# Scores and v of layer 1 by two levels of seven block products, with the outer additions done by adding transfers

## The chip, the cores and the metric

The kernel runs on one core of a Trainium2 chip. The metric is device microseconds (us) of one execution, all four layers on all eight images; lower is better. Before the change the median of three runs is 1862.45 us (1861.53 to 1862.72).

## The reference, cut to what matters

Four layers follow each other on x of shape (8, 512, 32, 32). An image is a matrix of C = 512 channels by N = 1024 positions. The change is in layer 1:

```
h = group_norm(x)                                  # 512 x 1024
q, k, v = wq h, wk h, wv h
attn = softmax(q^T k / sqrt(C), axis=-1)           # 1024 x 1024
x = x + wp (v attn^T)
```

Layer 0 is an attention without softmax whose result is a small matrix per image, layer 2 a softmax attention with 128 channels, layer 3 a product of signs with a scale and a slope.

## The kernel before

Weights are folded first: `wu` = wk-by-wq and `wo` = wp-by-wv, each 512 x 512, so layer 1 needs only u = wu h, the scores h^T u (one map of 1024 x 1024), v = h^T wo, and the values, v times the exponentials. All of these are float32 matmuls on the tensor engine (PE), with 128 rows contracted at a time.

Every big product is done by **seven block products in place of eight**. The operands are cut into quarters; `sums_of` (L337) makes the sums of one operand's quarters (A11, A12, A22, S1 to S4), `differences_of` (L353) the differences of the other's (B11, B21, B22, T1 to T4). `seven` (L366) runs the seven products and adds them up into the four result quarters: a result that is a partial sum is first moved out of PSUM by the scalar engine (ACT, `move`, L372) and later products are added to it by the vector engine (DVE, `plus`, L378).

Layer 1's u goes one level further since an earlier version: `make_u2` (L643) makes seven outer products, each of which `inner` (L594) does by seven smaller block products. The sums of the outer level are made by **adding transfers**: a DMA issued by GpSimd (POOL) with `accum_op=ALU.add` (L663) that adds one SBUF tile onto another. `prepare_u` (L576) makes the inner differences of h on POOL and loads the inner sums of wu, which `factors_of_u` (L561) has stored in HBM in batch 0.

The images are eight batches; `fast` (L1173) does one from layer 1's scores to layer 3. Its stages are, in order:

- `scores1` (L715): four groups of `seven` with two calls of 128x512 for each product, then exponentials on ACT and their column sums `esum` on DVE (L733 to L736);
- `make_v` (L698): two groups of `seven` with four calls of 128x256 for each product;
- `inverse_sums` (L1111): four narrow matmuls with ones add up `esum`, and the reciprocals go through HBM to all partitions;
- `values1` (L739): differences of the exponentials and sums of v on DVE, then 14 groups of four calls of 128x512; POOL adds results into xt (L769, L795);
- `project2` (L830), `scores2`, `values2`, `close2`, `leave`: layers 2 and 3. `make_u2` of the next batch is stepped between the matmuls of `project2` and `scores2`.

Into scores and v of a batch fall three other things: the second half of layer 3 of the batch before (`leave` in `rest3`), the loading of a further image, and `entering` (L1153), which runs layer 0's last product of the next image into it, with eight DVE additions (L460) and eight statistics (L463).

The order on PE is written out by hand: the stages are generators, and `fast` steps them one after another (`manual_schedule`). On the other engines a scheduler sets the order when the program is built[...]. POOL's DMA issues stand in POOL's order, plain DMAs in SyncE's (SP). [...]

Of the kernel before, what the change touches and what calls it, by code (L numbers as in the profile page):

```python
# [8 lines left out]
F32 = mybir.dt.float32  # L9
# [7 lines left out]
P = 128  # L17
# [70 lines left out]
def kernel(  # L88
# [55 lines left out]
    def half(i):  # L144
        return bass.ts(i, HF)
# [115 lines left out]
    fac_dram = [dram.tile([P, 7, P], F32, name=f"fac_dram{i}") for i in range(7)]  # L261
# [29 lines left out]
    wo = wpool.tile([P, CC, C], F32, tag="wo", name="wo")  # L291
# [5 lines left out]
    so = wpool.tile([P, 3, 2, C // 2], F32, tag="so", name="so")  # L297
# [214 lines left out]
    def make_u(env, hb, got, early=False):  # L512
# [4 lines left out]
        def done():  # L517
            us = env["big"].tile([P, 3, 2, HF], F32, tag="us", name="us")
            got.append(
                sums_of(quarters_of(ut, chunks, [half(0), half(1)]), [us[:, i] for i in range(3)])  # L520
            )
# [39 lines left out]
    def factors_of_u(env):  # L561

        tt = nc.gpsimd.tensor_tensor
        for i, (a, _) in enumerate(pairs):
            w = weights["u"][a]
            a11, a12, a21, a22 = (w[:, k, bass.ts(m, P)] for m in range(2) for k in range(2))
            s = env["small"].tile([P, 4, P], F32, tag="half_a", name="factors")
            tt(s[:, 0], a21, a22, ALU.add)
            tt(s[:, 1], s[:, 0], a11, ALU.subtract)
            tt(s[:, 2], a11, a21, ALU.subtract)  # L570
            tt(s[:, 3], a12, s[:, 1], ALU.subtract)
            nc.sync.dma_start(out=fac_dram[i][:, 0:2], in_=w[:, :, 0:P])
            nc.sync.dma_start(out=fac_dram[i][:, 2], in_=a22)
            nc.sync.dma_start(out=fac_dram[i][:, 3:7], in_=s)
            yield

    def prepare_u(env, hb, i):

        jit = env["jit"]
        fac = jit.tile([P, 7 + i % 2, P], F32, tag=f"fac{i % 2}", name="fac")  # L580
        nc.sync.dma_start(out=fac[:, 0:7], in_=fac_dram[turns[i]])
        b = hb[pairs[turns[i]][1]]
        t = jit.tile([P, 4, QF], F32, tag="jit", name="jit", bufs=2)
        lo, hi = slice(0, QF), slice(QF, HF)
        tt = nc.gpsimd.tensor_tensor
        for k in range(2):
            tt(t[:, k], b[:, k, hi], b[:, 0, bass.ts(k, QF)], ALU.subtract)  # L587
        tt(t[:, 2], b[:, 1, hi], t[:, 0], ALU.subtract)
        tt(t[:, 3], b[:, 1, lo], t[:, 2], ALU.subtract)
        rhs = {  # L590
            "B11": b[:, 0, lo],
            "B21": b[:, 1, lo],
            "B22": b[:, 1, hi],
            "T1": t[:, 0],  # L594
            "T3": t[:, 1],
            "T2": t[:, 2],
            "T4": t[:, 3],
        }
        return fac, rhs

# [50 lines left out]
    def make_u2(env, hb, got, made):  # L651
# [28 lines left out]
        for i, (d, bias, after) in enumerate(how):  # L680
            for j, _ in enumerate(inner(made[i], d, bias)):
                if j == 3:
# [4 lines left out]
                    if i == 6:  # L687
                        us = []
                        for tag, bufs in (("jit", 2), ("fac1", 1), ("jit", 2)):
                            x = env["jit"].tile([P, 2 * HF], F32, tag=tag, name="us", bufs=bufs)  # L690
                            us.append(x.rearrange("p (i n) -> p i n", i=2))
# [23 lines left out]
    def scores1(env, hb, ua, es):  # L715

        scale = float(C) ** -0.5
        esum = env["small"].tile([P, N], F32, tag="esum", name="esum", bufs=1)
        for i in range(NTH):
            lo, hi = (env["e"].tile([P, N], F32, tag="e", name="e") for _ in range(2))  # L720
            es[i], es[NTH + i] = lo, hi
# [5 lines left out]
            yield from seven(  # L727
                term, lo[:, half(0)], hi[:, half(0)], lo[:, half(1)], hi[:, half(1)], exp=scale
            )
            nc.scalar.activation(hi, hi, AF.Exp, scale=scale)  # L730
            nc.scalar.activation(lo[:, half(0)], lo[:, half(0)], AF.Exp, scale=scale)
            if i == 0:
                nc.vector.tensor_tensor(esum, lo, hi, ALU.add)  # L733
            else:
                nc.vector.tensor_tensor(esum, esum, lo, ALU.add)
                nc.vector.tensor_tensor(esum, esum, hi, ALU.add)  # L736
        es.append(esum)

    def values1(env, xt, vt, es, r, more):  # L739
# [8 lines left out]
        s2 = more[:, 0, :].rearrange("p (t c) -> p t c", c=w)  # L748
        t2 = more[:, 1:3, :].rearrange("p i (t n) -> p (i t) n", n=HF)
        e11, e12, e21, e22 = (  # L750
            [es[k * NTH + t][:, half(n)] for t in range(NTH)] for k in range(2) for n in range(2)
# [23 lines left out]
        for t in range(NTH):  # L775
            tt(e12[t], e22[t], e12[t], ALU.subtract)
            tt(t2[:, t, :], e12[t], e11[t], ALU.add)
# [10 lines left out]
        for t in range(NTH):  # L788
            tt(e11[t], e22[t], t2[:, t, :], ALU.subtract)
# [9 lines left out]
        for t in range(NTH):  # L799
            tt(e21[t], e21[t], t2[:, t, :], ALU.subtract)  # L800
        for i in range(2):
            pb = bank()
            group(pb, s2, [t2[:, t, :] for t in range(NTH)], i, True, True)
# [27 lines left out]
    def project2(env, xt, made):  # L831
# [3 lines left out]
        tpg = big.tile([P, 3, N], F32, tag="us", name="tpg")  # L835
        tt, pt = tpg[:, 0:1, :], tpg[:, 1:2, :]
        gt = tpg[:, 2, :].rearrange("p (t c) -> p t c", c=P)
# [273 lines left out]
    def inverse_sums(env, esum, row):  # L1111
# [4 lines left out]
        for q in range(g):  # L1116
            mm(
                out=ps[bass.ts(q, P // g), 0:w],
                lhsT=ones2[:, 0 : P // g],
                rhs=esum[:, bass.ts(q, w)],  # L1120
                start=True,
                stop=True,
                tile_position=(0, q * P // g),
            )
# [45 lines left out]
    rest3 = []  # L1170
    verdict = []

    def fast(env, n, hb, ua):  # L1173
# [11 lines left out]
        es = [None] * NT  # L1185
        for k, _ in enumerate(scores1(env, hb, ua, es)):
# [6 lines left out]
            if n == 0 and k == 2:  # L1193
                weights["o"] = sums_of(quarters_of(wo, chunks, cols2), [so[:, i] for i in range(3)], True)
            if n == 0 and k in (9, 11, 13, 15, 17, 19, 21):
                next(late_u)
            if n == 0 and k == 6:
                tp = quarters_of(sbw["tpg"], chunks, [slice(0, P), slice(P, 2 * P)])
                weights["tp"] = sums_of(tp, [sp[:, i] for i in range(3)], True)
            if k == 8 and more:  # L1200
                ahead = entering(n + 1)


            if k in (10, 13, 20, 27):
                next(ahead, None)
            chore(n == 0 and k in (1, 4, 7, 9, 11, 15, 17, 19, 23, 25))
        esum = es.pop()
        vt = env["big"].tile([P, NT, C], F32, tag="uv", name="vt")
        for k, _ in enumerate(make_v(hb, vt)):
            if k == 3:  # L1210
                r = inverse_sums(env, esum, n)
            if k == 5:
                next(ahead, None)
            chore(k in (1, 7, 10, 13) or n == 0 and k == 4)
        for _ in ahead:
            pass
        scratch = env["big"].tile([P, 3, N], F32, tag="us", name="scratch")
        got = []
        steps = iter(())
        for k, _ in enumerate(values1(env, xt, vt, es, r, scratch)):  # L1220
            chore(k in (2, 7, 9, 11, 13) or n == 0 and k in (8, 10, 12))
# [9 lines left out]
        signs = None  # L1231
        if more:
# [874 lines left out]
```

## Time and profile before

| | |
|---|---|
| median of three runs | 1862.45 us |
| the profiled execution | 1861.81 us |
| its span, first to last instruction | 1859.9 us |
| granted PE clock | 0.999 |
| PE busy | 1840.3 us (99%) |
| DVE, ACT, POOL busy | 1183.0, 569.6, 382.1 us |
| 128x512 float32 matmuls of values1 (L756), 768 + 128 | 336.9 + 56.2 us busy |
| 128x512 matmuls under L427 of layer 1's scores (ut and us with h and hs), 384 + 256 + 128 + 128 | 178.9 + 115.6 + 60.3 + 60.3 us busy |
| 128x256 matmuls under L427 of v (wo and so with h and hs), 384 + 256 + 128 + 128 | 90.1 + 59.3 + 31.0 + 30.2 us busy |
| adding transfers, 28 of 512 KB and 42 of 256 KB | 25.7 MB |

A group of the profile is a line, an engine, an operation and the tiles that it writes and reads; `bank<-ut,h 128x512 x384` are 384 PE instructions that write a PSUM bank from tiles ut and h. Matmuls overlap, so the mean duration of one (594 ns with 512 columns) is longer than what one more adds to the time. Idle time of an engine that isn't the bound costs nothing. The span is 1.9 us shorter than the execution's own time.

### The profile page before, as it was taken

The numbers are of one execution on the slowest core, as the hardware profiler recorded it, in microseconds if no ns is written. First come the engines' busy times: TensorE is split into PE (matmuls) and PEld (weight loads), VectorE is DVE, ScalarE is ACT, GpSimd is POOL, SyncE is SP. The second block draws the span as 40 slices with busy tenths as digits, with TensorE's granted clock in tenths as the row PEclk, the third lists the DMA queues.
The fourth block names the chain that finished last, engine by engine and source line by source line (L and its number), as shares of the span: only waits on it lengthen the run. The fifth ranks groups of instructions, "written<-read, shape, count | busy, mean of one in ns | idle before, by whom it ended". The sixth has DMA issues, their size and how long they took to land.

```text
span 1859.9 us, 18071 instructions
## 1 busy us (share of the span) xinstructions
PE 1840.3 (99%) x6504; PEld 1001.1 (54%) x6504; DVE 1183.0 (64%) x2191; ACT 569.6 (31%) x1020; POOL 382.1 (21%) x402
## 2 busy tenths in 40 slices
PE   9999999999999999999999999999999999999997
PEld 3365464644656465644646455644646464644653
DVE  3357788567765768567765776467654767365547
ACT  2042221344213521244214521244213521344113
POOL 1002103420224003420234003420324004410011
PEclk9999999999999999999999999999999999999999
DMA  8640100342006200242006210242006200330001
GB/s 286 200 138 24 43 18 1 72 98 86 12 10 129 102 27 1 63 100 93 14 8 131 90 40 1 64 99 89 12 10 131 100 22 1 84 79 23 12 1 47
DMA packets 57532, 119.05 MB, mean 64 GB/s; under 512 B 7200, under 2 KB 17244, under 8 KB 57180
## 3 DMA queue, kind: packets, MB, share of 16 engines
q1 hardware_dynamic: 42844, 91.70, 15.1%
q0 software_dynamic: 13728, 25.70, 8.0%
q8 instruction: 53, 0.87, 0.2%
q10 hardware_dynamic: 864, 0.43, 0.1%
q14 instruction: 43, 0.35, 0.1%
HBM read 68.92 MB, written 23.20 MB: 50 GB/s over the span
## 4 chain that ended last, share of the span: by engine, by line
PE 86%; DVE 4%; ACT 4%; issue 4%; DMA 1%; POOL 0%; DVEq 0%; POOLq 0%; ACTq 0%; SPq 0%
PE bank L427 34%; PE bank L756 20%; PE bank L611 8%; PE bank L1095 6%; PE bank L1257 5%; PE bank L1648 4%; PE bank L857 3%; PE bank L876 2%; PE bank L451 1%; ACT sg L887 1%; PE bank L899 1%; ACT both L940 1%; DVE both L920 1%; ACT up L939 1%; ACT e L372 1%
## 5 line engine op out<-in xcount | busy, mean ns | idle before, releaser
L756 PE MATMUL bank<-e,vt 128*128 128x512 f32 x768 | 336.9, 594 | 0.0
L756 PEld LDWEIGHTS bank<-e,vt 128*128 128x128 f32 x768 | 144.1, 190 | 170.9 <-issue 165.7
L427 PE MATMUL bank<-ut,h 128*128 128x512 f32 x384 | 178.9, 600 | 2.1 <-ACT e L372 1.4
L249 POOL TENSOR_TENSOR r_r<-r_v,minus_half 128x4 f32<-128x4 f32 (+1 forms) x11 | 11.0, 1000 | 767.4 <-DVE r_v L248 761.8
L1095 PE MATMUL bank<-tpg 128*128 128x512 f32 x256 | 126.0, 592 | 0.0
L427 PEld LDWEIGHTS bank<-ut,h 128*128 128x128 f32 x384 | 70.3, 190 | 98.8 <-issue 82.6
L611 PE MATMUL bank<-jit,fac 128*128 128x256 f32 x392 | 117.1, 380 | 0.1
L1257 PE MATMUL bank<-e,tpg 128*128 128x512 f32 x256 | 115.8, 595 | 0.0
L427 PE MATMUL bank<-us,hs 128*128 128x512 f32 x256 | 115.6, 593 | 0.0
L1102 ACT ACTIVATE e<-bank 128x512 f32<-128x512 f32 x128 | 76.5, 597 | 96.3 <-PE bank L1095 96.3
L378 DVE TENSOR_TENSOR e<-bank,e 128x512 f32<-128x512 f32 x96 | 66.1, 689 | 62.1 <-PE bank L427 46.9
L611 PEld LDWEIGHTS bank<-jit,fac 128*128 128x128 f32 x392 | 70.6, 190 | 54.1 <-issue 45.3
L587 POOL TENSOR_TENSOR jit<-h 128x256 f32<-128x256 f32 x56 | 49.9, 910 | 199.6 <-PE bank L611 112.6
L427 PE MATMUL bank<-wo,h 128*128 128x256 f32 x384 | 90.1, 384 | 0.0
L372 ACT COPY e<-bank 128x512 f32<-128x512 f32 x96 | 55.7, 581 | 102.2 <-PE bank L427 102.1
L427 PEld LDWEIGHTS bank<-us,hs 128*128 128x128 f32 x256 | 48.4, 190 | 59.8 <-issue 59.6
L1257 PEld LDWEIGHTS bank<-e,tpg 128*128 128x128 f32 x256 | 48.1, 190 | 58.1 <-issue 56.9
L427 PEld LDWEIGHTS bank<-wo,h 128*128 128x128 f32 x384 | 71.3, 190 | 12.6 <-issue 3.8
L378 DVE TENSOR_TENSOR vt<-bank,vt 128x512 f32<-128x512 f32 x48 | 33.2, 692 | 64.7 <-PE bank L427 63.8
L372 ACT COPY vt<-bank 128x512 f32<-128x512 f32 x64 | 37.4, 584 | 117.5 <-PE bank L427 117.4
L887 ACT ACTIVATE sg<-xt,rb 128x512 f16<-128x512 f32 x60 | 40.9, 717 | 101.2 <-DVE xt L878 98.4
L628 ACT COPY ut<-bank 128x256 f32<-128x256 f32 x126 | 46.9, 372 | 80.7 <-PE bank L611 79.4
(407 smaller groups left out, 3326.5 us busy)
## 6 DMA issues: line engine op xcount, KB each, us to landing
xt<-in_x SPq DMA_DIRECT2D x55, 512.0 KB
fac<-fac_dram SPq DMA_DIRECT2D x49, 448.0 KB
out<-both SPq DMA_DIRECT2D x63, 256.0 KB
ut<-ut POOLq DMA_DIRECT2D x28, 512.0 KB, 5.0
ut<-p POOLq DMA_DIRECT2D x42, 256.0 KB, 5.3
rfull<-r_dram SPq DMA_DIRECT2D x15, 512.0 KB
f_dram<-f SPq DMA_DIRECT2D x8, 256.0 KB
fb<-f_dram SPq DMA_DIRECT2D x8, 256.0 KB
```

The lines of the kernel that those rows point to most:

```text
L372: nc.scalar.copy(dst, ps)
L378: nc.vector.tensor_tensor(dst, ps, u, ALU.add)
L427: mm(out=ps[:, q * w : (q + 1) * w], lhsT=lt(ka, kb, q, k), rhs=rhs(ka, kb, q, k), start=first and q == 0 and k == 0, stop=last and k == 1 ...
L587: tt(t[:, k], b[:, k, hi], b[:, 0, bass.ts(k, QF)], ALU.subtract)
L611: mm(out=out, lhsT=fac[:, blocks[a], :], rhs=rhs[b], start=first, stop=last, skip_group_check=True,)
L756: mm(out=ps, lhsT=a[:, t, bass.ts(r_, P)], rhs=e[t], start=first and t == 0, stop=last and t == NTH - 1, skip_group_check=True,)
L857: mm(out=ps[:, i, :], lhsT=xt[:, cc, bass.ts(4 * h + i, P)], rhs=sbw["tpg"][:, cc, 2 * P : 3 * P], start=cc == 0, stop=cc == CC - 1,)
L887: nc.scalar.activation(sg[:, cc, :], xt[:, cc, half(h)], AF.Sign, bias=rb3[:, cc : cc + 1])
L1095: mm(out=ps, lhsT=pt[:, 0, bass.ts(t, P)], rhs=tt[:, 0, half(h)], start=True, stop=True,)
L1102: nc.scalar.activation(e[:, half(h)], ps, AF.Exp, scale=float(P) ** -0.5)
L1257: mm(out=banks[h], lhsT=gt[:, t, :], rhs=es[t][:, half(h)], start=t == 0, stop=t == NT - 1,)
L1648: one = mm(out=banks[i][side(h), :], lhsT=w0[i][:, cc, :], rhs=xt[:, cc, half(h)], start=cc == 0, stop=cc == CC - 1,)
```

## The change

For the seven batches after batch 0, `scores_and_v` takes the place of `scores1` and `make_v`. Batch 0 keeps these two; in it `factors_of` (the old `factors_of_u` with a name) also stores the inner sums of `wo` in HBM (`facv_dram`).

Scores are seven outer products ("units" 0 to 6) of seven inner ones each, v units 7 to 13. A step is one inner product: two calls, of 256 columns for the scores, of 128 for v. The steps of a unit are called a0, c3, a2, c4, b1, a5, a6: the letter is the PSUM bank that they use (a holds a running sum of four products), the figure the inner product. After each step the result is moved to the unit's destination by ACT (a0, c3, a2, a6) or added to it by DVE (c4, b1, a5). In units 6 and 13 DVE adds all seven to what is there. `WIDE` and `NARROW` set how the steps of neighbouring units interleave on PE.

A unit's destination is a quarter of the result (C11 to C22) or a spare (X, Y). `hooks` says after which step which outer addition is issued: `add` is an adding transfer on POOL's queue, 13 for the scores (eleven of 512 KB, two of 256 KB) and 8 for v (256 KB), `sum_v` a DVE addition, `exp` an exponential, `total` a part of the column sums, on DVE for the first and on POOL for the other five. Quarters of the exponentials now lie in tiles of two row blocks each, so that one transfer covers two.

The right-hand operands of the scores and left-hand ones of v are the inner differences of h, which `prepare_u` has made for u anyway: they are kept (`hb2`), in a tile for each of the seven, and one of four is made in place. `prepare_s` makes the inner sums of u on POOL, two units ahead, `load_factors` loads those of `wo`. `values1` works on the new tiles with 128x1024 DVE operations in place of pairs of 128x512. `inverse_sums` takes two sums in place of one for layer 1. Some tiles move between pools to make room; `wo` is stored in HBM for the fallback at the end.

```diff
     def prepare_u(env, hb, i):
 
-        jit = env["jit"]
-        fac = jit.tile([P, 7 + i % 2, P], F32, tag=f"fac{i % 2}", name="fac")
-        nc.sync.dma_start(out=fac[:, 0:7], in_=fac_dram[turns[i]])
...
-        t = jit.tile([P, 4, QF], F32, tag="jit", name="jit", bufs=2)
+        k = turns[i]
+        fac = load_factors(env, fac_dram[k])
+        b = hb[pairs[k][1]]
+        t = env["jit"].tile([P, 3, QF], F32, tag=f"turned{k}", name="turned")
...
-        for k in range(2):
-            tt(t[:, k], b[:, k, hi], b[:, 0, bass.ts(k, QF)], ALU.subtract)
-        tt(t[:, 2], b[:, 1, hi], t[:, 0], ALU.subtract)
-        tt(t[:, 3], b[:, 1, lo], t[:, 2], ALU.subtract)
+        tt(t[:, 0], b12, b11, ALU.subtract)
+        tt(b12, b22, b12, ALU.subtract)
+        tt(t[:, 1], b22, t[:, 0], ALU.subtract)
+        tt(t[:, 2], b21, t[:, 1], ALU.subtract)
...
+    def prepare_s(env, ua, i):
+
+        u = ua[STURNS[i]]
+        s = env["jit"].tile([P, 7, P], F32, tag="fac", name="summed", bufs=3)
...
+        tt(s[:, 0], a21, a22, ALU.add)
+        tt(s[:, 1], s[:, 0], a11, ALU.subtract)
+        tt(a21, a11, a21, ALU.subtract)
+        tt(s[:, 2], a12, s[:, 1], ALU.subtract)
...
+        plan = {
+            "a0": ("a", 0, True, False, move, d11),
+            "c3": ("c", 3, True, False, move, d22),
+            "a2": ("a", 2, False, False, move, d12),
+            "c4": ("c", 4, False, True, plus, d12),
+            "b1": ("b", 1, True, True, plus, d11),
+            "a5": ("a", 5, False, False, plus, d22),
+            "a6": ("a", 6, False, True, move, d21),
+        }
...
+    WIDE = {"a0": 0, "c3": 2, "b1": 3, "a2": 4, "c4": 6, "a5": 8, "a6": 12}
+    NARROW = {"a0": 0, "c3": 1, "a2": 3, "c4": 4, "b1": 5, "a5": 6, "a6": 9}
...
+    def products_of(lt, rhs, w):
+
+        def product(ps, k, first, last):
+            a, b = pairs[k]
+            for q in range(2):
+                mm(
+                    out=ps[:, q * w : (q + 1) * w],
+                    lhsT=lt[b][:, bass.ts(q, P)],
+                    rhs=rhs(a),
+                    start=first and q == 0,
+                    stop=last,
+                    skip_group_check=True,
+                )
...
+        s_dst = (C22, C11, C12, C21, C22, X, C12)
+        v_dst = (X, C12, C22, C11, C21, Y, C12)
...
+        hooks = {
+            (1, "a5"): [add(es_of, C11, C22, 1)],
+            (1, "a6"): [add(es_of, C11, C22, 0)],
+            (2, "a5"): [add(es_of, C12, C22, 1), add(es_of, C12, C22, 0, lo)],
+            (2, "a6"): [add(es_of, C12, C22, 0, hi)],
+            (3, "a0"): [exp(C11, 1, 0)],
+            (3, "b1"): [exp(C11, 1, 1)],
+            (3, "a5"): [add(es_of, C21, C12, 1), exp(C11, 0, 0)],
+            (4, "a0"): [exp(C11, 0, 1)],
+            (3, "a6"): [add(es_of, C21, C12, 0)],
+            (4, "c4"): [total(0, (C11, 0), (C11, 1))],
+            (4, "a5"): [add(es_of, C12, C22, 1)],
+            (4, "a6"): [add(es_of, C12, C22, 0)],
+            (5, "c4"): [add(es_of, C22, C21, 1)],
+            (6, "a0"): [add(es_of, C22, C21, 0)],
+            (6, "a2"): [add(es_of, C21, X, 1), exp(C22, 1, 0)],
+            (6, "c4"): [exp(C22, 1, 1)],
+            (6, "a5"): [add(es_of, C21, X, 0)],
+            (7, "a0"): [exp(C22, 0, 0)],
...
+            (9, "a5"): [add(v_of, C22, C12, 1), exp(C21, 0, 0)],
+            (9, "a6"): [add(v_of, C22, C12, 0)],
...
+            (10, "a5"): [add(v_of, C11, X, 1)],
+            (10, "a6"): [add(v_of, C11, X, 0)],
+            (12, "c3"): [add(v_of, C21, C22, 1)],
+            (12, "c4"): [add(v_of, C21, C22, 0)],
+            (12, "a5"): [sum_v(C12, Y, 1)],
+            (12, "a6"): [sum_v(C12, Y, 0)],
+            (13, "a5"): [add(v_of, C22, Y, 1), add(v_of, C22, Y, 0)],
+        }
...
+        else:
+            last_v = scores_and_v(env, ua, ua_made, es, sv)
+            for k in range(37):
+                next(last_v)
+                last_rest(k)
+                if k == 8 and more:
+                    ahead = entering(n + 1)
+                if k in (9, 12, 17, 22, 30):
+                    next(ahead, None)
+                chore(k in (28, 35))
+                if k == 33:
+                    r = inverse()
```

## The prediction, made before the changed kernel was run

> **What bounds the kernel now.** I read busy shares first, then the chain of work that ended last, then groups of instructions, then the stage that the change rewrites (the last 60 us of a batch's scores and v) in the windows view.
>
> ```profile
> PE 1840.3 (99%) x6504; PEld 1001.1 (54%) x6504; DVE 1183.0 (64%) x2191; ACT 569.6 (31%) x1020; POOL 382.1 (21%) x402
> ...
> PE 86%; DVE 4%; ACT 4%; issue 4%; DMA 1%; POOL 0%; DVEq 0%; POOLq 0%; ACTq 0%; SPq 0%
> ```
>
> TensorE (PE) is busy 99% of the span and holds 86% of the chain; weight loads run beside it. So PE's instructions, times what each adds to the chain, are the time. What each adds is read from runs of equal matmuls on the chain in order of time (start, us, what):
>
> ```profile
> 1721.96 17.46 PE bank L427 x80
> 1739.42 48.07 PE bank L756 x112
> ...
> 1799.51 7.14 PE bank L857 x64
> ```
>
> One matmul with 256 columns adds 17.46/80 = 0.2183 us, with 512 columns 48.07/112 = 0.4292, with 128 columns 7.14/64 = 0.1116. Each matmul call of the program is two such instructions: values1 makes 56 calls, and the chain counts 112. All three prices are proportional to columns, so a narrow product wastes nothing, with a new weight tile in each call.
>
> ```profile
> 1463.00:1537.40 74.40, 73.95 (x248) 42.19 (x247) 48.00 (x82) 28.12 (x44) 1.10 (x2) 1.00 0.18 60
> ```
>
> This is scores and v of one batch (from:to, length, then busy us of PE, PEld, DVE, ACT, POOL, clock, DMA share, GB/s): PE never waits, DVE has 26 us to spare, GpSimd (POOL) is empty and DMA is busy 18%. It is this slack that the change spends.
>
> ```profile
> q0 software_dynamic: 13728, 25.70, 8.0%
> ...
> ut<-ut POOLq DMA_DIRECT2D x28, 512.0 KB, 5.0
> ...
> DMA to landing us min/median/max: 3.4/5.1/7.4
> ```
>
> These price an adding transfer, which the kernel already uses for u: 512 KB land 5.0 us after issue; over all (the third line, 256 and 512 KB) 3.4 to 7.4. Their queue moves 25.70 MB in 8.0% of 1859.9 us, 173 GB/s.
>
> [...] POOL waits 15.0 us in six places for ut<-p before it issues the next add to the same rows. [...] the 128x1024 subtraction of L360 takes 1.74 us at 1340.7, beside POOL, and 1.22 at 1376.6, with POOL idle.
>
> **The change, part by part** (unit numbers from 0, as in the hooks).
>
> *Products.* Scores took 4x7x2 = 56 calls of 512 columns, 112 instructions, 112 x 0.4292 = 48.07 us; v 56 calls of 256, 24.45 us. Two levels make 49 products of two calls, 196 instructions: scores at 256 columns 42.79, v at 128 columns 21.87. That is 5.28 + 2.58 = 7.86 us per batch, for seven batches -55.0. Bounds: the prices are those of unbroken streams, so only a wait can spoil them.
>
> *inverse_sums.* Two sums per quarter: 16 instructions for 8. The 8 lasted 1519.14 to 1519.71, 0.57 us; eight batches, +4.6.
>
> *Adding transfers.* 13 adds for the scores (6.3 MB) and 8 for v (2.1 MB) per batch: 8.4/173 GB/s = 49 us of DMA, factors for v 3.2 MB at the plain queue's 327 GB/s (91.70 MB in 15.1%) another 10, and 13 (18% of 74) are there: 72 us of DMA in a stage of some 70. So DMA goes from idle to full, and the adds depend on each other. The order of the built program shows the chain that decides, each waiting on the landing before it: C21+=C12 half 1 after (3,a5); C12+=C22 half 1; C12+=C22 half 0, queued on POOL behind C22+=C21 half 1, which waits for the previous; then VectorE's add of (6,a0) into C12, for which PE's (6,a2) waits; then C22+=C21 half 0; C21+=X half 0; its exponential, and behind that on ScalarE the copy of (8,a0), for which PE's (8,a2) waits.
>
> One add costs 5.0 us less the shorter issue: 256 rows took POOL 1.19 us, 128 rows 0.86 at the least, and the new adds have 128 rows: p = 4.7. From the end of (3,a5) as 0: VectorE first has seven instructions of the next batch's entry (4 x 0.73, 3 x 0.68, begun about 3.7 before) and its own 0.69, so the first add is issued at 3.0, lands 7.7; second 7.7 to 12.4; C22's is issued, 0.9, then the third 13.3 to 18.0; VectorE 0.8, so (6,a2) can start at 18.8. PE reaches it after 16 steps of 4 x 0.2183 = 0.873 and the entry's 1.92 us, at 15.9: a stall of 2.9. Fourth 18.0 to 22.7, fifth to 27.5, two exponentials of 0.63 and a copy of 0.37: 29.2. PE would reach (8,a2) at 19 x 0.873 + 9 x 0.446 + 2 x 0.873 + 1.92 = 24.3. Total stall 4.9 us per batch. With p = 3.4 (the least landing, 128 rows of half the bytes: right if rows, not bytes, set the cost) it is about 0.3; with p = 5.8, two adds and a factor load in flight together, 10.4. It can't gain. I take 4.7, since plain transfers with 4 KB rows and with 2 KB rows both run near 330 GB/s here (286 GB/s at share 0.86 in the first slice), which speaks for bytes.
>
> *VectorE, ScalarE.* In v's 22 us VectorE has 25 adds of 0.42, four sums of 0.69, four 128x1024 ones of 1.22 moved ahead from values1, a reciprocal of 1.75 and some 3 us of small ones: 23. Between (u,a5) and (u,a6) it has only 0.9 us. Bounds 0 to 3 us per batch; I take 1.0. ScalarE has 24 copies of 0.37 and twelve exponentials of 0.63, 16.5 us: room, apart from the wait priced above.
>
> *POOL.* Per batch 5 preparations of 4 operations at 0.73 to 1.2, 21 issues at 0.9 to 1.2, ten sums near 1.3: about 53 us in 70; it had 1.1. Queued behind its waits are the later adds alone, counted above, and the sums, which inverse_sums needs some 10 us later: 0. The seven prepare_u now all run under values1, 28 operations for 35 before, ahead of POOL's additions into xt; they end about 30 us into its 48 while xt's first late addition comes at 32: 0, up to 2 if VectorE is slowed throughout.
>
> *Edits at nothing.* factors_of for o: 28 POOL operations of 0.55 to 0.78 and 21 small stores in batch 0, under its scores and v, and needed one batch later; the 1 MB store of wo; pools moved; esum's VectorE additions gone (8.6 us where it had slack). If that cover is gone, 0 to 4 us once.
>
> *Sum.* 1861.8 (profiled execution) - 55.0 + 4.6 + 7 x (4.9 + 1.0) = 1852.7; that execution is 0.6 below the median, so 1853.
>
> **Rivals.**
> *Adds in time (1818).* p = 3.4: 1861.8 - 50.4 + 7 x 1.0. For: rows halve per byte. Against: 5.0 in the page at the same bytes.
> *The chain of adds becomes the bound (1894, slower).* At p = 5.8 the stall is 10.4 + 1.5: 1861.8 - 50.4 + 83. For: the DMA sum above, 7.4 us as longest landing, where four were in flight. Against: PE's stall itself gives transfers time. It decides from p = 5.0 on, where 7 x (6.2 + 1.0) eats the 50.4.
> *Narrow matmuls cost more (1960).* Were 128 columns bound by a weight load's 0.19 us: 196 x 0.078 x 7 = 107. L857's 0.1116 speaks against it.
>
> **How the numbers follow.** 0.2% (3.7 us) is about what a measurement can tell from no change. Forecast, 1842 to 1858, 0.38; adds in time, down to 1815, 0.20; between 1858.7 and 1866.2, 0.08, the crossing of forecast and second rival; chain as bound, 1866 to 1900, 0.32; narrow matmuls 0.02. Faster 0.58, same 0.08, slower 0.34. Range 1820 to 1888 leaves 0.06 below and 0.14 above; the forecast's own range is 1842 to 1858.
>
> **What would show it.** Products: runs of 196 instructions at 0.2183 and 0.1116. The chain: PE waiting in scores for VectorE at (6,a2), released by an adding transfer, about 3 us, and for ScalarE at (8,a2), about 2 us; median landing of the 512 KB adds of e against 4.7. DMA share near 0.9 in that stage. The forecast is wrong if landings are under 4 or over 5 us, if values1's first groups wait for v's last adds, or if VectorE, with no transfer behind it, holds v by more than 3 us.

## The result, and the profile after

The changed kernel takes 2097.36 us (median of four runs, 2095.38 to 2101.47) against 1862.23 of the kernel before (four runs): a ratio of 1.1266, 95% interval 1.1246 to 1.1286. It is slower, by 235 us, and lies far outside the 1820 to 1888 of the prediction. The profiled execution took 2101.47 us, its span is 2099.6.

The head of the page of the changed kernel: busy us, share of the span and instructions of each engine, and the clock that TensorE was granted, in tenths, over 40 slices.

```profile
PE 1872.0 (89%) x7744; PEld 1174.2 (56%) x7744; DVE 1280.0 (61%) x2343; ACT 641.3 (31%) x1248; POOL 845.7 (40%) x843
...
PEclk9999999998999889998999979998899889998999
```

TensorE fell from 99% to 89% busy, and its clock, 9 in every slice before, has digits of 7 and 8. The chain of work that ended last can't be followed in this trace (its shares come out as 0%), so the rest is read from waits and timelines. Who TensorE waited for, in the changed kernel (us in total, times, longest):

```profile
PE bank L667 <- DVE vt L631: 76.9, 21, 7.6
PE bank L667 <- ACT e L637: 62.1, 7, 11.1
PE bank L667 <- DVE e L631: 46.7, 7, 7.5
PE bank L667 <- ACT vt L637: 13.0, 7, 2.7
```

L667 is the matmul of the new products, L631 and L637 the two ways a product leaves its bank (`plus` and `move` of `unit`). These four rows are 199 us, 28 us a batch. In the kernel before, scores and v had one such row:

```profile
PE bank L427 <- ACT e L372: 1.4, 4, 0.4
```

TensorE's timeline in one batch of the changed kernel shows them (start, us, what; in brackets the idle time ahead and who ended it):

```profile
1426.76 2.05 PE L667 MATMUL bank<-summed,h 128*128 128x256 f32 x4 [7.80 <-ACT e L637]
1428.74 3.78 PE L454 MATMUL bank<-fb,pv 64*128 64x512 f32 x8
1432.45 1.13 PE L667 MATMUL bank<-us,hs 128*128 128x256 f32 x4
...
1456.70 2.05 PE L667 MATMUL bank<-summed,turned 128*128 128x256 f32 x4 [6.32 <-DVE e L631]
...
1468.81 0.71 PE L667 MATMUL bank<-fac,turned 128*128 128x128 f32 x4 [1.56 <-ACT vt L637]
...
1478.48 2.08 PE L667 MATMUL bank<-fac,turned 128*128 128x128 f32 x8 [6.72 <-DVE vt L631]
1480.35 3.50 PE L667 MATMUL bank<-fac,h 128*128 128x128 f32 x16
1483.69 1.50 PE L667 MATMUL bank<-fac,turned 128*128 128x128 f32 x12
...
1502.99 2.93 PE L667 MATMUL bank<-fac,h 128*128 128x128 f32 x12 [5.82 <-DVE vt L631]
```

Call them gap A (7.80, in the scores), gap B (6.32, at the seventh product of the scores), gap C (6.72) and gap D (5.82), both in v. Behind each of them the same matmuls take longer: four of 256 columns 2.05 us, elsewhere 1.03; sixteen of 128 columns 3.50, elsewhere 1.95. The windows view of these stretches (from:to, length, busy us of PE, PEld, DVE, ACT, POOL, then the granted clock, DMA share, GB/s) says why:

```profile
1426.70:1431.00 4.30, 4.24 (x10) 2.37 (x12) 0.84 (x2) 0.90 (x2) 3.03 (x4) 0.50 0.80 194
1456.70:1460.10 3.40, 3.40 (x10) 2.80 (x11) 1.34 (x2) 0.00 (x0) 0.28 (x1) 0.56 1.03 193
1478.40:1483.70 5.30, 5.22 (x25) 5.22 (x26) 3.83 (x8) 0.74 (x2) 0.00 (x0) 0.51 0.27 87
1502.90:1508.00 5.10, 5.01 (x16) 3.74 (x17) 2.70 (x7) 2.04 (x2) 0.04 (x1) 0.55 0.52 85
```

TensorE is busy there, and its granted clock reads 0.50 to 0.56 over these stretches. Behind the four large gaps of this batch, 5.8 to 7.8 us long, the clock of 0.50 lasts 3.0 to 5.6 us into the work; behind the gap of 1.56 it stays at 1.00. Shorter gaps than those four have it too: of the five between 2.2 and 2.8 us in this trace, four were followed by 2.8 to 3.4 us of work at 0.50. One of them, and the clock behind it:

```profile
738.26 0.71 PE L667 MATMUL bank<-fac,turned 128*128 128x128 f32 x4 [2.74 <-ACT vt L637]
```

```profile
739.50:742.90 3.40, 3.17 (x16) 2.88 (x14) 3.37 (x3) 1.15 (x4) 3.40 (x3) 0.50 0.00 0
```

So a gap of 2.74 us was followed by 3.4 us of it as well.

The account of this batch closes. From its first product of the scores to its first matmul of values1 the kernel before took 81.1 us and the changed one 111.9. My products and sums alone would give 81.1 - 7.9 + 0.6 = 73.8, so 38.1 us have to be found. The gaps (7.80, 6.32, 1.56, 6.72, 0.66, 5.82) are 28.9. Half clock cost, as the time each stretch took less the same matmuls at full rate: 5.69 - 2.79, 3.42 - 1.90, 5.21 - 2.68 and 7.05 - 4.77, together 9.2. Sum 38.1. Over the whole run it is much the same: TensorE's gaps of more than 0.1 us add up to 216 us (8 before), and it is busy 142 us at half clock, which costs half of that, 71 (an estimate, from four matmuls taking 2.05 us there and 1.03 elsewhere). Of the 290 us between this execution and my sum without any stall (2101.5 and 1811) that is 279.

What the gaps wait for stands one queue further on. ScalarE at gap A in the changed kernel:

```profile
1422.34 1.15 ACT L758 ACTIVATE e<-e 128x512 f32<-128x512 f32 x2 [5.24 <-DMA e<-e]
1426.03 1.56 ACT L637 COPY e<-bank 128x512 f32<-128x512 f32 x3 [2.54 <-DMA out<-both]
```

Two exponentials (L758) wait 5.24 us for an adding transfer; the copy that TensorE needs stands behind them, and then waits 2.54 more, because its tile takes the place of an output tile of the batch before whose store hasn't landed. VectorE at gaps C and D:

```profile
1470.26 5.91 DVE L1025 TENSOR_TENSOR e<-e 128x1024 f32<-128x1024 f32 x1 [3.84 <-POOL acc L775]
1476.20 1.23 DVE L1026 TENSOR_TENSOR scratch<-e 128x1024 f32<-128x1024 f32 x1
1477.34 1.08 DVE L631 TENSOR_TENSOR vt<-bank,vt 128x256 f32<-128x256 f32 x3
...
1501.38 1.23 DVE L1027 TENSOR_TENSOR vt<-vt 128x1024 f32<-128x1024 f32 x1 [4.49 <-DMA vt<-vt]
1502.52 0.42 DVE L631 TENSOR_TENSOR vt<-bank,vt 128x256 f32<-128x256 f32 x1
```

L1025 to L1028 open values1, the next stage, and have been moved ahead. L1025 waits for GpSimd's sum of the exponentials it overwrites, L1027 for the last adding transfer of v, and v's evictions (L631) stand behind them. But L1025's wait was over at 1470.26, before TensorE ran out of work at 1471.75. Most of gap C is L1025's own time, 5.91 us where it takes 1.22 elsewhere (the second L1025 at 1478.34). GpSimd was at its sums until 1475.07:

```profile
1465.16 9.91 POOL L775 TENSOR_TENSOR acc<-e,acc 128x512 f32<-128x512 f32 x8
```

The prediction had read the same, smaller, on L360: 1.74 us beside GpSimd, 1.22 with GpSimd idle. That GpSimd's sums make L1025 longer is likely, but no run changed them alone. With 1.22 us for L1025, gap C would be about 2.0 us (an estimate: 6.72 less 5.91 - 1.22). The evictions kept their place in VectorE's queue: three follow within 1.1 us behind L1026, and none comes ahead of it. Only gap B is the chain that the prediction priced.

### The profile page after: what moved, and what is told of

It reads as the page before. It is cut to its first block, busy times and chain, and to the rows that moved or that the text cites. A ratio compares the mean times of both kernels' runs of the same rounds, so it can differ in the third digit from the quotient of the medians.

```text
span 2099.6 us, 22031 instructions
## 1 busy us (share of the span) xinstructions
PE 1872.0 (89%) x7744; PEld 1174.2 (56%) x7744; DVE 1280.0 (61%) x2343; ACT 641.3 (31%) x1248; POOL 845.7 (40%) x843
## 3 DMA queue, kind: packets, MB, share of 16 engines
q0 software_dynamic: 43856, 84.42, 23.2%
q8 instruction: 63, 1.03, 0.2%
## 5 line engine op out<-in xcount | busy, mean ns | idle before, releaser
L631 DVE TENSOR_TENSOR e<-bank,e 128x512 f32<-128x512 f32 x154 | 105.1, 686 | 131.9 <-PE bank L667 83.9
L667 PE MATMUL bank<-summed,turned 128*128 128x256 f32 x392 | 108.5, 402 | 46.7 <-DVE e L631 46.7
L743 POOL DMA_DIRECT2D e<-e x77 | 71.9, 972 | 171.6 <-ACT e L637 68.9
L667 PE MATMUL bank<-fac,turned 128*128 128x128 f32 x588 | 91.7, 299 | 52.9 <-DVE vt L631 39.7
L667 PEld LDWEIGHTS bank<-fac,turned 128*128 128x128 f32 x588 | 81.1, 208 | 64.9 <-DVE vt L631 42.9
L667 PE MATMUL bank<-fac,h 128*128 128x128 f32 x448 | 82.0, 341 | 38.2 <-DVE vt L631 37.2
L667 PEld LDWEIGHTS bank<-summed,turned 128*128 128x128 f32 x392 | 77.5, 201 | 61.6 <-issue 50.8
L637 ACT COPY e<-bank 128x512 f32<-128x512 f32 x140 | 78.9, 582 | 101.5 <-PE bank L667 81.5
L758 ACT ACTIVATE e<-e 128x512 f32<-128x512 f32 x112 | 66.4, 627 | 112.0 <-DMA e<-e 91.7
L667 PEld LDWEIGHTS bank<-fac,h 128*128 128x128 f32 x448 | 75.8, 251 | 41.6 <-DVE vt L631 38.2
L667 PE MATMUL bank<-summed,h 128*128 128x256 f32 x112 | 40.2, 494 | 62.1 <-ACT e L637 62.1
L844 PE MATMUL bank<-turned,fac 128*128 128x256 f32 x294 | 87.7, 380 | 0.0
L775 POOL TENSOR_TENSOR acc<-e,acc 128x512 f32<-128x512 f32 x56 | 75.6, 1506 | 0.0
```

The costliest lines, as they stand in the source:

```text
L631: nc.vector.tensor_tensor(dst, out, dst, ALU.add)
L637: nc.scalar.copy(dst, out)
L667: mm(out=ps[:, q * w : (q + 1) * w], lhsT=lt[b][:, bass.ts(q, P)], rhs=rhs(a), start=first and q == 0, stop=last, skip_group_check=True,)
L743: nc.gpsimd.dma_start(out=of[x][i][:, :, cols], in_=of[y][i][:, :, cols], accum_op=ALU.add)
L758: nc.scalar.activation(e, e, AF.Exp, scale=scale)
L775: eng.tensor_tensor(accs[h][:, j], a[:, j], b[:, j], ALU.add)
```

## The experiments

Theories, from that reading. *L, landings*: the adding transfers are late, and whoever uses their sums is late in any order. *Q, queues*: what costs is an instruction that waits for a transfer or for GpSimd with evictions behind it. *P, products*: the narrow matmuls cost more than I priced. Times are medians; the kernel before took 1861.6 to 1862.4 beside them. All but the last are single executions, against differences of tens of us.

**1. One part at a time.**

*pin_values*: the opening of values1 held behind v's evictions on VectorE.

```diff
-            tt(p12[i], p22[i], p12[i], ALU.subtract)
-            tt(p2[i], p12[i], p11[i], ALU.add)
-        tt(a21, a11, a21, ALU.subtract)
-        tt(s2, a22, a21, ALU.subtract)
+            keep(tt(p12[i], p22[i], p12[i], ALU.subtract))
+            keep(tt(p2[i], p12[i], p11[i], ALU.add))
+        keep(tt(a21, a11, a21, ALU.subtract))
+        keep(tt(s2, a22, a21, ALU.subtract))
```

> Only the order on VectorE is changed: the six opening subtractions and additions of values1 (lines 1025 to 1028) are held behind v's evictions. Theory Q (queues: an instruction that waits for a transfer or for GpSimd's sums stands ahead of v's evictions on VectorE): the two gaps of TensorE in v, 6.7 and 5.8 us in one batch and 3.8 and 4.4 us in the next, and the half-clock stretches behind them (about 4 us a batch) go, 13 to 16 us a batch in seven batches, so about 1985 to 2010 us; part may come back as a wait in front of values1's products. Theory L (landings: the adding transfers are late in any order, values1 needs their sums at once): the gaps only move from v to the start of values1, 2080 us or more. Theory P (the narrow products cost more than priced): no change, 2097.

Measured 2068.54. TensorE's waits in pin_values (its lines are one further down than in the changed kernel):

```profile
PE bank L1006 <- DVE o_b L1072: 41.7, 6, 7.7
PE bank L667 <- DVE vt L631: 23.2, 18, 4.2
```

The waits of v fell from 76.9 to 23.2, as Q said, but 41.7 came back in values1, where there had been 4.4. There VectorE holds a subtraction for the next stage (L361) ahead of values1's eviction, and L361 waits for GpSimd, whose additions to xt stand behind prepare_u's 28 operations. The time lies between Q's 2010 and L's 2080. Q had allowed for something coming back in front of values1's products; this came later in values1, from a wait that had moved into a third queue.

*no_adds_s*: the transfers among the score tiles not issued, so the scores lack these additions.

```diff
             def do():
+                if of is es_of:
+                    return
                 nc.gpsimd.dma_start(
```

> The adding transfers among the tiles of the scores are left out (the twelve of each batch; the scores lack these additions), everything else stands. Theory L: both gaps in the scores (7.8 to 11.1 us for ScalarE's copy, 6.3 us for VectorE's addition), the half-clock stretches behind them (about 4 us) and, since the exponentials and GpSimd's sums come earlier, part of the first gap in v go: 20 to 28 us a batch, 1900 to 1955 us. Theory Q says the same for the scores, but the second gap of v (a21 behind its own transfer) stays at 4 to 6 us. If the first gap is instead the wait of ScalarE's copy for the stores of the last half (out<-both) it stays at about 5 us or more, and the time at about 1960 to 1990. Theory P: above 2050.

Measured 1942.88: 22 us a batch, within the numbers of both L and Q. In one batch the largest gap left in the scores is 2.65 us, and gap D is still 7.25: that it stays was Q's mark.

*scores_only* and *v_only*: one stage in two levels, the other by the code of before (`make_v` driven from the event loop in place of the second seven units; `scores1` ahead of the second seven units alone). Other operands stand in for those that the two levels would share, so the values differ.

> Two levels for the scores alone; v by one level as before the change, with the projection weights of layer 2 in place of its own and h's blocks as the operands of u left them (so v holds other values). If the stalls of the two stages are their own and add up: v's gaps and slow stretches go (about 14 us a batch), its dearer products come back (2.6 us a batch): about 2015 us. With v alone in two levels then about 1985 to 2000. If the first gap of v comes from GpSimd's sums of the exponentials it stays here at about 4 to 7 us and the time is about 2050.

> Two levels for v alone; the scores by one level as before the change, on blocks of h as the operands of u left them (other values). The gaps of the scores and their slow stretches (18 to 21 us a batch) go, the dearer products of the scores come back (5.3 us a batch): about 1985 to 2000 us if the stalls of the stages add up. The first gap of v (VectorE behind GpSimd's sums) cannot occur, since the sums are the old ones on VectorE; the second (a21 behind a transfer) can: if it stays, about 1930; theory P would have v cost more than the 24.5 us of before even outside the gaps.

Measured 2043.25 and 1982.91. In scores_only TensorE still loses 45.2 us in v, VectorE having waited 50.4 for GpSimd's sums in seven places, as the third case said. In v_only it loses 45.3 in v, most of it at gap D (9.5 us in one batch, VectorE waiting 8.1 for vt<-vt), and 25.9 in values1; its time is near the 1985 of stages that add up, but not for that reason. The losses over before, 181 and 121 us, add to more than 235, so the two stages share some.

**2. All queues in written order, and two suspects.**

*order_all*, *order_dve*: written order on the other engines too, on all three (the edit shown) or on VectorE alone.

```diff
-        with tc.manual_schedule(engines={mybir.EngineType.PE}):
+        with tc.manual_schedule(engines={mybir.EngineType.PE, mybir.EngineType.Pool, mybir.EngineType.DVE, mybir.EngineType.Activation}):
```

> Only the order of issue is changed: in the eight passes over the batches VectorE, ScalarE and GpSimd, like TensorE, issue in the order in which the code was written, so nothing that waits for a transfer or for GpSimd is hoisted ahead of an eviction, and the 28 operations of prepare_u no longer stand ahead of values1's additions to xt on GpSimd. Theory Q (hoisted work in the queues): v's two gaps, the gap in values1 that replaced them when only lines 1025 to 1028 were held back (6 us), and the part of the first gap of the scores that ScalarE's early exponentials make (about 5 us) go, with about 6 us of half clock: some 20 us a batch, 1930 to 1980 us. Theory L (late landings in any order): the gap at the seventh product of the scores (6.5 us) and the wait for out<-both stay, and others appear where the sums are used: 2030 us or more. Written order may lose elsewhere, where the scheduler had done well; then the gaps of v are gone and new ones stand in other stages.

> Written order on VectorE alone (and TensorE, as before). Theory Q: v's gaps go as with lines 1025 to 1028 held back, and the new gap in values1 (VectorE's L361 for the next stage hoisted ahead of the eviction while it waits for GpSimd) goes too: 2069 less 6 to 8 us a batch, 2010 to 2030 us. The gaps in the scores stay as they are (7.8 to 11 and 6.5 us). Theory L: as with those lines alone, 2060 us or more.

Measured 2127.66 and 2182.61: both slower than the changed kernel, which neither theory had said; L's open ranges (2030 or more, 2060 or more) only happen to hold them. TensorE's waits in order_all:

```profile
PE bank L667 <- ACT e L637: 57.7, 21, 4.2
PE bank L667 <- DVE vt L631: 52.8, 17, 7.4
PE bank L1125 <- DVE att L1546: 44.2, 8, 6.3
PE bank L667 <- DVE e L631: 36.0, 13, 4.4
```

New waits of 44.2 us came in layer 2 (L1125), and 52.8 in v are left. In order_dve v's waits for VectorE fell to 23.5, but those in the scores rose from 46.7 to 124.5. So Q as I had put it, that the scheduler's hoists are the fault, falls. Written order has its own instructions that wait with others behind them; what counts is which wait stands ahead of which eviction.

*store_apart*: output tiles of the last half in other buffers.

```diff
+                elif j == 0:
+                    both = small.tile([P, 2, HF], F32, tag="rfull", name="both", bufs=1)
...
+                else:
+                    y1, y2 = (
+                        small.tile([P, HF], F32, tag="half_b", name="both") for _ in range(2)
+                    )
```

> The two output tiles of a batch's last half are put into buffers that the scores don't use (rfull and half_b) in place of the pool of score tiles. If ScalarE's first copy into the fourth pair of score tiles waits last for the stores out<-both (it started 2.5 and 3.7 us after the exponentials ahead of it), the first gap of the scores shrinks by 2.5 to 4 us a batch: 2070 to 2080 us, and the exponentials' wait for the adding transfer is left as its cause. If the exponentials alone set it: 2090 to 2100. If the stores were all of it: gap gone, 2030 to 2045.

Measured 2068.56. TensorE's wait for ScalarE's copies of scores fell from 62.1 us to

```profile
PE bank L667 <- ACT e L637: 22.2, 7, 4.7
```

The store was the last thing that gap A waited for; the exponentials are left.

*adds_dve*: the same additions on VectorE.

```diff
+                if of is es_of:
+                    t = of[x][i][:, :, cols]
+                    nc.vector.tensor_tensor(t, t, of[y][i][:, :, cols], ALU.add)
+                    return
```

> The adding transfers among the tiles of the scores are done by VectorE at the places where they were issued (about 1.2 us each for 128x1024 in place of 6.6 us to landing); the sums are the same. Theory L (the landing time of a transfer in a chain is the cost): both gaps in the scores go as when the additions were left out (1943 us), VectorE's 12 additions of about 14 us a batch lie beside TensorE or cost a few us a batch: 1945 to 1985 us. If VectorE is the bound instead, with these in its queue: 2000 to 2040. If the gaps come from waits other than the landings: 2060 or more.

Measured 2035.43, in the second case. VectorE's load shows as small gaps in the scores (24.0 us in 19), but 31.0 at gap A and 61.6 in v stay as well. Both this run and no_adds_s take the same transfers away, so the 93 us between them come from the additions on VectorE: ScalarE's exponentials now wait 70.6 us for them (L745), in 32 places.

**3. The named waits together.** *pins_store* is pin_values and store_apart, with two more holds: prepare_u's operations on GpSimd, and the next stage's subtractions (L361) on VectorE.

```diff
-        tt = nc.gpsimd.tensor_tensor
+        def tt(*a):
+            tc.keep_in_program_order(nc.gpsimd.tensor_tensor(*a))
...
-            [env["e"].tile([P, 2, HF], F32, tag="e", name="xd") for i in range(4)],
+            [env["e"].tile([P, 2, HF], F32, tag="e", name="xd") for i in range(4)],
+            True,
```

> Three queues are put right by name and nothing else: lines 1025 to 1028 behind v's evictions and the next stage's subtractions (L361 for xd) behind values1's on VectorE, prepare_u's operations in their written place on GpSimd, and the last half's output tiles out of the score tiles. Theory N (named waits, each of its own): 2097 less 29 (stores, measured), less 29 (lines 1025 to 1028, measured), less the 6 us gap in values1 that the latter brought (7 x 6 = 42): about 1997, 1985 to 2015; the gap at the seventh product of the scores (6.4 us) stays. Theory W (whatever is put right, the wait moves to the next late transfer): 2040 or more.

Measured 2000.41, against 1997. Four waits named from the trace and put right together are worth 97 us, as N's sum said; of its parts two were measured alone (29 each), and the third (42) is an estimate. TensorE's wait at the seventh product stays, 52.5 us.

*pins_store_ahead*: order of the units 0 to 5, 7, 8, 6, 9 to 13, with the exponentials moved to match.

> As pins_store, and the first two products of v are done ahead of the last one of the scores, some 6 us of TensorE between the chain of adding transfers and the eviction that waits for it. Theory N: the 6.4 us gap and its half clock of about 2 us go, 7 x 8 = 58 us: about 1940. Theory W: the exponentials and GpSimd's sums, now later against v, wait instead: within 15 us of pins_store.

It tells little: I had put one exponential ahead of the last addition to its tile, the values grew, and the kernel's own guard ran its general path behind the fast one (4308.17 in all). In the fast part six batches, from values1 to values1, took 225 to 236 us against 224 to 234 of pins_store, and a gap of 6.8 us stood at ScalarE's copies of v in place of gap B, behind exponentials that wait for transfers. That speaks for W, with this reserve.

*pins_store_adds_dve* and *pins_store_no_adds*:

> As pins_store, with the twelve additions among the scores on VectorE in place of transfers. Theory N: alone it gave 62 us; less what the store fix has in common with it: 1940 to 1965. If VectorE (some 75 us of work in a stage of 75 us) is the bound: 1970 or more, with many small gaps of TensorE in the scores.

> As pins_store, with all 22 adding transfers of a batch in scores and v left out (scores and v lack these additions), so that no wait for a landing is left there. It prices the products and evictions of the new form alone. If my prices of the products hold (1861.8 less 55.0, plus 4.6 for the sums): 1812 to 1845. If narrow products or VectorE's narrow evictions cost more than the sum said: 1870 or more.

Measured 1939.31, just under N's range and with small gaps of TensorE in the scores (34.5 us in 20), and 1864.37, between the two cases (the hooks issue 21 such transfers a batch, not 22). The latter, TensorE over a stretch of 200 us (columns as above):

```profile
1240.00:1440.00 200.00, 195.84 (x823) 127.29 (x822) 133.60 (x200) 72.28 (x141) 87.11 (x82) 1.00 0.26 73
```

98% busy at full clock, and its scores and v take 75 to 78 us in the first six of these batches, 80 to 82 before. P falls: the products cost what the sum said (7.3 us a batch less than before) within some 3 us a batch, 1.6 of them waits for VectorE's evictions of v. The 1864 isn't lower because the stretch between values1 and the next scores is 3 to 8 us longer a batch (5.0 in the mean), with VectorE's held operations in it. Everything else between this and 2000 is the adding transfers and the waits for them.

**4. What is left of the additions.** *pins_store_chain*: four of the twelve on VectorE (`sum_s` is adds_dve's addition).

```diff
-            (4, "a5"): [add(es_of, C12, C22, 1)],
-            (4, "a6"): [add(es_of, C12, C22, 0)],
+            (4, "a5"): [sum_s(C12, C22, 1)],
+            (4, "a6"): [sum_s(C12, C22, 0)],
```

(and so for C21 and C12 at (3,a5) and (3,a6)).

> As pins_store (2000), with the four chained additions of the scores alone (C21+=C12 and the second C12+=C22) on VectorE, the other eight still by transfers. If the landing of that chain is what the seventh product waits for, its gap (7.5 us a batch) and the half clock behind it (3 to 4 us) go for four additions of 1.2 us: 2000 less 7 x 10 = 70, about 1930, 1915 to 1945. If VectorE's load decides, it gains less than 40: 1960 or more.

*pins2_store_chain_exp*: without the hold on L361, exponentials of C11 written one unit later.

> As pins_store_chain, with the four exponentials of C11 one unit later in ScalarE's order, and the next stage's subtractions on VectorE left to the scheduler again (they cost some 5 us a batch after values1 where held back). If ScalarE's queue is what is left in the scores: 3 to 5 us a batch, and about 4 for the other: 1930 less 7 x 8 = 56, about 1875, 1860 to 1895. If VectorE waits for GpSimd in values1 again without the hold, 1915 or more.

Measured 1967.83 and 1955.13; both fall short. TensorE's wait at gap B, in pins_store and in pins_store_chain:

```profile
PE bank L674 <- DVE e L638: 52.5, 10, 7.5
```

```profile
PE bank L674 <- DVE e L638: 8.0, 8, 2.1
```

So the chain's gap went, and VectorE's load isn't what decides, though the time lies in that range: 31.2 us stood at ScalarE's copies of x: exponentials of C22 that wait for their transfers stand ahead of them. The second run changed nothing there, because the scheduler put the later exponentials back in their old place; its 13 us are those of L361.

*exp_pin* holds the exponentials where they are written, one or two units later; *exp_pin_8* also puts the additions to C11 and the first to C12 on VectorE.

```diff
-                nc.scalar.activation(e, e, AF.Exp, scale=scale)
+                tc.keep_in_program_order(nc.scalar.activation(e, e, AF.Exp, scale=scale))
```

> As pins2_store_chain_exp (1955), with the exponentials held in their written place on ScalarE and C11's and C22's one or two units later, so that no copy of the scores stands behind an exponential that waits for a transfer. If that queue made the gaps (4.6 us, 1.3 and 2.0 us at ScalarE's copies) with 2 us of half clock: 1955 less 7 x 8 to 10, 1885 to 1900. If the copy into C22 waits for the transfers that read it, the 4.6 us gap only moves by a few products: 1935 or more. Sums on GpSimd come later against v and could hold values1's opening: 1910 to 1935.

> As exp_pin, with the four first additions (C11+=C22 and C12+=C22) on VectorE too, eight of the twelve; only C22+=C21 and C21+=X stay transfers. If transfers that read C22 were the cause: 15 to 45 us below exp_pin, 1875 to 1900. If VectorE's load decides: 5 to 25 us above exp_pin.

Measured 1924.27 and 1919.40. The first lies in the range of the third case, but values1's opening holds nothing up; the second is 5 us below the first, which neither case said. TensorE's waits for ScalarE are nearly gone (in exp_pin 8.1 us at its copies of scores, under 1 at those of x), and the next one shows. VectorE in exp_pin:

```profile
1369.45 0.16 DVE L250 TENSOR_TENSOR r_e<-r_r 128x4 f32<-128x4 f32 x1 [6.63 <-POOL r_r L249]
```

The next batch's normalisation needs a power of four columns from GpSimd, which stands behind ten sums of the exponentials, now later; v's evictions stand behind L250.

*pow_early*: that step called earlier.

```diff
-                if k in (9, 12, 17, 22, 30):
+                if k in (9, 12, 17, 22, 26):
```

> As exp_pin_8 (1919), with the second half of the next batch's normalisation (its matmul, the power on GpSimd at line 249 and VectorE's chain behind it) issued four steps earlier. If the 5.6 us gap in v is VectorE waiting for that power behind the sums: it and 2 us of half clock go, 1919 less 7 x 7 = 49, about 1870, 1860 to 1885; below 1862 only if nothing else comes up. If the sums, now later, hold the matmuls of inverse_sums or values1's opening instead: 1895 or more.

Measured 1902.92 (median of four), ratio to before 1.0219, interval 1.0202 to 1.0237: better by 17, not by 49; the time lies in the second case's range, but its waits (inverse_sums, values1's opening) are under 1 us. The gap shrank from 5.6 to 3.5 us. VectorE in pow_early:

```profile
1345.19 0.16 DVE L253 TENSOR_TENSOR r_r<-r_r,r_e 128x4 f32<-128x4 f32 x1
1345.39 1.12 DVE L485 TENSOR_TENSOR r_r<-r_r,ct 128x4 f32<-128x4 f32 x1
1346.55 1.19 DVE L487 TENSOR_TENSOR bi<-mean,r_r 128x4 f32<-128x4 f32 x1
```

An operation on four columns takes 0.16 us, and the next two 1.12 and 1.19, each time until the end of the GpSimd sum then running (1345.22 to 1346.50, 1346.46 to 1347.72).

No version beat the kernel before. Of the 235 us, 194 were taken back. The last 41 seem to lie in small waits for VectorE in scores and v (23.7 and 27.7 us in pow_early) and in the held operations. I didn't try to remove these.

## Why the prediction was wrong

- *Products, -55.0*: right as far as the runs tell. Where TensorE isn't kept waiting, matmuls go at the old prices: in the batch shown, 32 of 256 columns from 1433.42 to 1440.33 add 0.216 us each and sixteen of 128 columns from 1489.30 to 1491.09 add 0.112, for 0.2183 and 0.1116. And in pins_store_no_adds scores and v are 4 to 7 us a batch shorter than before, where products and sums said 7.3. *inverse_sums, +4.6*: not tried apart; it fits the account of the batch.
- *Chain of adds, 2.9 at (6,a2)*: right place, wrong size: 46.7/7 = 6.7 us. The term is p = 4.7. In the batch shown the three chained adds are issued at 1436.5, 1442.2 and 1449.0 (behind C22's at 1448.5), and by the trace's records of their semaphores they land 5.2, 5.8 and 6.9 us later; then VectorE goes on. From a landing to the next issue it is 0.5 and 1.1 us, where I had 0 and 0.9. That makes 19.4 us where the sum had 15.0. Landings in the changed kernel (number, KB each, median us):

```profile
e<-e POOLq DMA_DIRECT2D x63, 512.0 KB, 6.6
...
e<-x POOLq DMA_DIRECT2D x14, 512.0 KB, 4.9
```

and in exp_pin_8, where two e<-e a batch are left, issued 7 us apart (1334.37, 1341.30), and two e<-x that follow at 1343.09 and 1346.39, in company:

```profile
e<-e POOLq DMA_DIRECT2D x14, 512.0 KB, 4.9
e<-x POOLq DMA_DIRECT2D x14, 512.0 KB, 7.1
```

  So 4.7 was about the price of one add alone, and I used it for adds whose two halves, factor loads and stores are in flight together. That company is the cause is not shown: no run changed it by itself, the e<-x of the changed kernel land in 4.9, and C22's add, issued 0.5 us ahead of the third chained one, landed in 4.8. The second stall, 2.0 at (8,a2), came as said: 13.0/7 = 1.9. My 72 us of DMA a batch were right (a share of 0.67 over 111.9 us is 75); the share near 0.9 didn't come, because the stage had grown.
- *VectorE and ScalarE, 1.0 (0 to 3)*: the step that failed most. I counted "four 128x1024 ones of 1.22 moved ahead from values1" as 1.22 us of work each. I left out what each waits for, with v's evictions behind, and that the first would take 5.91 beside GpSimd's sums (in four of the seven batches), though I had read L360's 1.74 for 1.22: 11.0 us a batch in v (76.9/7). "ScalarE ... room, apart from the wait priced above" missed gap A, 62.1/7 = 8.9 us: exponentials of C11 ahead of the copies, and the store of an output tile. Shown by pin_values, store_apart, exp_pin.
- *POOL, 0*: wrong twice. Queued behind its waits were not "the later adds alone": besides inverse_sums L1025 waits for the sums, since it overwrites what they read, and the power of the next batch stands behind them (exp_pin, pow_early). The hoisted prepare_u did delay additions to xt, 38.7 us of ScalarE's wait for GpSimd in values1, though TensorE lost only 4.4 by it until gap C was closed.
- *Half clock*: not in the sum at all; 9.2 us a batch in the one taken apart and 71 us over the run, a quarter of the loss in both.
- *Rivals*: the second, a chain that becomes the bound (its 5.8 us for a landing was assumed, with no reading given for it), had the right sign and a fifth of the loss: gap B with the half clock behind it is 7 x (6.7 + 1.5) = 57 us of the 286 between 2097 and 1811, my sum without any stall. The third fell with P. My tests "if VectorE, with no transfer behind it, holds v by more than 3 us" and "landings over 5 us" both came true.

A gap closed alone gave less than it was worth. pin_values took 53.7 us of waits out of v and gained 29, since waits in values1 rose from 4.4 to over 40; store_apart took 39.9 out of the scores and gained 29, since waits for VectorE rose by 11.6. Likely each gap had given the transfers, sums and stores behind it time to land, and with one closed TensorE comes earlier to the next; no run tests this by itself.

## What to carry to other kernels

When work moves from an engine that is full to queues that are half empty, price what each moved instruction waits for, what stands behind it in its queue and who runs beside it, not its busy time alone; here a hoisted operation priced at 1.22 us took 5.91, and TensorE's gap behind it was 6.72. List for every late result all its readers, those that overwrite it and those that only reuse its buffer included. And count a stall of the bound engine twice where the trace shows it: in the batch taken apart TensorE's gaps were 28.9 us and the slow stretches behind them cost 9.2 more.

## What the hardware showed beyond that

- In the batch taken apart TensorE's four gaps of 5.8 to 7.8 us were followed by 3.0 to 5.6 us of work at a granted clock of 0.50, worth 1.5 to 2.9 us each; in the same trace four of five gaps of 2.2 to 2.8 us were followed by 2.8 to 3.4 us of it.
- While GpSimd ran eight sums back to back (1465.16 to 1475.07), VectorE's L1025, a 128x1024 subtraction with two SBUF inputs begun at 1470.26, took 5.91 us in place of 1.22 and ended 1.1 us after the last sum. So it was in four of the seven batches (5.91 to 5.93 us); in the other three the same operation took 2.28 or 2.29 and ended with sums still running (in one, at 740.68, with GpSimd at its sums until 745.24). In pow_early L485 and L487, on four columns, took 1.12 and 1.19 us beside sums, where in exp_pin L487 took 0.16. What decides between these cases was not shown.
